# Moving the matrix transposes of a gated graph network from TensorE to 16-bit DMA transposes joined on ScalarE

## The chip, the core and the metric

The kernel runs on one core of a Trainium2 chip. The core has a matrix engine (TensorE, in the profile PE, with its weight loads shown as PEld), a vector engine (VectorE, DVE), an activation engine (ScalarE, ACT), a general engine (GpSimd, POOL) and a queue that here only issues DMAs (SyncE, SP). All engines run at once, each takes its own instructions strictly in order, and semaphores tie them together. The metric is the device time of one launch in microseconds (us); lower is better. Before the change it is 2248.63 us, the median of three runs between 2247.92 and 2249.76.

## What is computed

A batch of 64 graphs, each with 256 nodes and 256 features per node, goes through two layers. The first is a gated graph network with three rounds of message passing, the second an attention layer. Both see a normalized input and add their result to it.

```python
# x: (64, 256, 256) f32; adj: (64, 256, 256) int32, about 3% ones
h = relu(layernorm(x))
A = (adj != 0)
for i in range(3):                                   # layer 0
    m    = h @ weight[i]
    aggr = einsum('bst,bsd->btd', A, m)              # sum over source nodes
    gi, gh = aggr @ w_ih.T + b_ih, h @ w_hh.T + b_hh
    r = sigmoid(gi_r + gh_r);  z = sigmoid(gi_z + gh_z)
    n = tanh(gi_n + r * gh_n)
    h = (1 - z) * n + z * h
x = x + h
h = relu(layernorm(x))                               # layer 1
h1 = h @ W.T
e = leaky_relu((h1 @ a_left)[:, :, None] + (h1 @ a_right)[:, None, :])
alpha = softmax(where(adj == 0, -1e9, e))
out = x + alpha @ h1
```

Two layouts of the state h are needed. The gate products contract over features, so they need h with features on the partitions. Message passing contracts over source nodes, so it needs h with nodes on the partitions. Between rounds the state must therefore be transposed, as must the attention weights before they multiply h.

## The kernel before

Two graphs form a pair, and 32 pairs are worked one after the other, up to four of them open at once (WINDOW). A tile is 128 partitions by 512 f32 columns (256 KB): 28 general tiles ("full"), 32 of the rounded type fp32r ("round"), and the eight banks of PSUM. The names in the profile are these classes.

For each pair the stages are:

- Loading x and adj, layernorm and relu (`norm_relu`), and splitting the node-layout state into a rounded part hi and a remainder lo, so that message passing (`prop`, L541) runs as two fp32r products. Before round 0 the normalized state is also transposed into feature layout (`turn`, L523) and copied out of PSUM by ScalarE (L527).
- Three rounds. In each, the feature-layout state (hT, one tile for each of two feature blocks) and the propagated sum are cut into three rounded pieces by `split` (L440 to L443). Twelve or six matmuls of 128x512 for each gate and feature block follow in `gate`: the "top" products (L456), a scaling of the bank by ScalarE (L470), then the "rest" products (L461). Each round has 72 such matmuls for a pair, 36 for each feature block. Sigmoid, tanh and the update of hT in place (L572 to L574) follow on ScalarE and VectorE.
- After each round, the updated hT is transposed back to node layout (`back`, L584), for each graph four 128x128 transposes into one bank. After rounds 0 and 1, ScalarE rounds the bank to hi (L591) and VectorE forms lo (L592); after round 2, VectorE adds the bank to x (`res`, L589).
- Layernorm of the result and attention: scores, mask, exponential (L633). The weights are transposed by TensorE (`p turn`, L648), copied out (L652), multiplied by the state (`mix`, L657), projected (L666), scaled and added, and stored.

No engine's order is written by hand. Every operation is recorded in a `Plan` with an engine, an occupancy and a latency in ns, and the buffers that it reads and writes. `Plan.run` walks a clock and always places the operation that can start first; ties go by priority, which is a due time minus a hand-set lead (`LEAD`). The order so found is what each engine's queue holds. `in_turn` keeps the gates in a fixed interleaving: round 0 of pair p, round 2 of pair p-1, round 1 of pair p, round 0 of pair p+1, and so on. A wrong cost makes no wrong result, only another order. The occupancy constants of the plan are `MM, TR, PROP, PASS = 432, 109, 120, 232` and `A512, V512, S512, VP256, C512 = 470, 605, 660, 395, 530`; TR is one 128x128 transpose and PASS one 128x512 matmul. A DMA occupies SP in the plan for 5.6 ns per KB and lands 2200 ns later.

Of the kernel before, what the change touches and what calls it, by code (L numbers as in the profile page):

```python
# [10 lines left out]
F32 = mybir.dt.float32  # L11
F32R = mybir.dt.float32r
I32 = mybir.dt.int32
AF = mybir.ActivationFunctionType
# [9 lines left out]
    "w load": 3000, "load": 1000, "w 1": -20000, "G": -27000, "in 0 stats": -8000, "in 0 shift": 28000,  # L24
    "turn 1": 20000, "prop 0": -1000, "g1 d": -12000, "r 0 topF": 20000, "nh 0 topF": 4000, "ni 0 topF": 3000,
    "ni 0 rest": 9000, "z 0 topF": -6000, "z 0 rest": -3000, "r 1 topT": 1000, "nh 1 topF": -4000,
    "ni 1 topF": -5000, "z 1 topF": -22000, "back 0": 15000, "lo 0": -6000, "lo 1": 11000, "mid 0 stats": -15000,
    "mid 0 relu": -8000, "dot 0": -7000, "right 0": -15000, "project 0": -10000,
# [16 lines left out]
class Plan:  # L45
# [79 lines left out]
    def run(self, deadline):  # L125
# [16 lines left out]
        while done < len(self.ops):  # L142
            best = None
            for e, (free, avail) in engines.items():
                for o in avail:
                    if o.pair >= oldest + self.window and o.pair > 0:
                        continue
                    t = free
                    for q in o.preds:
                        t = max(t, q.start + q.occ if q.eng == e else q.end)  # L150
                    if o.port:
                        t = max(t, port["POOL" if e == "DVE" else "DVE"])
                    fits = True
                    for b in o.bufs:
                        if b.slot is None:
                            f = [s[0] for s in self.slots[b.cls] if s[2] is None]
                            if len(f) <= self.keep.get(b.cls, 0) * max(0, o.pair - max(oldest, 0)):
                                fits = False
                                break
                            t = max(t, min(f))  # L160
                    if fits and (best is None or (t, o.prio, o.seq) < best[0]):
                        best = ((t, o.prio, o.seq), o)
# [30 lines left out]
def tile_gated_gnn_then_gat(  # L193
# [82 lines left out]
    def dma(name, kb, fn, **kw):  # L276
        plan.op(name, "SP", kb * 5.6, kb * 5.6 + 2200, fn, **kw)
# [196 lines left out]

    def norm_relu(name, src, dst):
# [25 lines left out]
    def pair(p):  # L501
# [15 lines left out]
        for db in range(DB):  # L517
# [10 lines left out]

        for i in range(L):
# [4 lines left out]
            for db in range(DB):  # L534
                pa, ag = Buf("bank"), Buf("full")

                def prop(db=db, pa=pa, hi=hi, lo=lo):
                    for g in range(G):
                        terms = [(part[g], sb) for part in (hi, lo) for sb in range(NB)]
                        for n, (b, sb) in enumerate(terms):  # L540
                            nc.tensor.matmul(pa.t[:, ts(g, N)], parts(b)[:, sb, ts(db, P)], parts(A[g])[:, sb, :],  # L541
                                             start=(n == 0), stop=(n == len(terms) - 1))

                pe(f"prop {db}", 8 * PROP, prop, r=[(b, ONE) for b in hi + lo + A], w=[(pa, ONE)])
# [30 lines left out]

            if not last:
                hi, lo = [Buf("round") for _ in range(G)], [Buf("round") for _ in range(G)]
            for g in range(G):
                pt = Buf("bank")

                def back(g=g, pt=pt, hT=hT):
                    for nb in range(NB):
                        for db in range(DB):
                            nc.tensor.transpose(pt.t[:, (nb * DB + db) * P : (nb * DB + db + 1) * P],  # L584
                                                parts(hT[db])[:, g, ts(nb, P)], ident)

                pe(f"back {g}", 4 * TR, back, r=[(b, (g,)) for b in hT], w=[(pt, ONE)])
                if last:
                    dve(f"res {g}", V512, lambda b=XR[g], pt=pt: nc.vector.tensor_add(b.t, b.t, pt.t), r=[(pt, ONE)], w=[(XR[g], ALL)])  # L589
                else:  # L590
                    act(f"hi {g}", A512 + 10, lambda b=hi[g], pt=pt: nc.scalar.copy(b.t, pt.t), r=[(pt, ONE)], w=[(hi[g], ONE)])  # L591
                    dve(f"lo {g}", V512, lambda b=hi[g], c=lo[g], pt=pt: nc.vector.tensor_sub(c.t, pt.t, b.t.bitcast(F32)),  # L592
                        r=[(pt, ONE), (hi[g], ONE)], w=[(lo[g], ONE)])
# [45 lines left out]
        for g in range(G):  # L639
# [3 lines left out]
            pt, pT, pg, ag, pv = Buf("bank"), Buf("full"), Buf("bank"), Buf("full"), Buf("bank")  # L643

            def turn(g=g, pt=pt):
                for jb in range(NB):
                    for ib in range(NB):
                        nc.tensor.transpose(pt.t[:, (jb * NB + ib) * P : (jb * NB + ib + 1) * P],  # L648
                                            parts(pm_[g])[:, ib, ts(jb, P)], ident)

            pe(f"p turn {g}", 4 * TR, turn, r=[(pm_[g], ALL)], w=[(pt, ONE)])
            act(f"p copy {g}", A512, lambda pt=pt, pT=pT: nc.scalar.copy(pT.t, pt.t), r=[(pt, ONE)], w=[(pT, ONE)])  # L652

            def mix(g=g, pT=pT, pg=pg):
                for db in range(DB):
                    for jb in range(NB):
                        nc.tensor.matmul(pg.t[:, ts(db, N)], parts(hb[g])[:, jb, ts(db, P)], pT.t[:, ts(jb, N)],  # L657
                                         start=(jb == 0), stop=(jb == NB - 1))

            pe(f"mix {g}", 4 * MM, mix, r=[(pT, ONE), (hb[g], ALL)], w=[(pg, ONE)])  # L660
# [50 lines left out]
```

## Time and profile before

| | before |
|---|---|
| median of three runs | 2248.63 us |
| profiled execution, device time | 2247.52 us |
| its span, first to last instruction | 2245.7 us |
| one pair, span / 32 | 70.2 us |
| TensorE clock granted | 0.996 |

The profiled execution lies 1.1 us under the median, and its span 1.8 us under its own device time. A line of the groups reads: source line, engine, operation, output<-inputs by tile class, shape, xcount | busy us in total, mean ns of one | idle time just before, and what ended it. "Busy" of TensorE includes the drain of each matmul, so instructions that follow each other overlap: the distance from one start to the next, not the mean duration, is what one costs. In the timeline the columns are the start in us, the time from the first start to the last end of the group, engine, line, operation and count.

### The profile page before, as it was taken

To read this page: it belongs to the slowest core of one execution; us is meant where nothing else is said; L and a number is where in the kernel's file an instruction comes from. 1 tells how busy PE (TensorE), PEld (TensorE's weight loads), DVE (VectorE), ACT (ScalarE), POOL (GpSimd) and SP (SyncE) were. 2 spreads that over 40 slices of the span, in tenths; PEclk is the share of its full clock that TensorE was granted. 3 is DMA by queue.
4 is the path that set the end of the run, shared out by engine and by line. 5 is a ranking of instruction groups with operands and counts; after the bars stand their busy time and mean duration, and the time that the engine had idled before them with its cause. 6 is when DMAs were issued, how large, how long until landed. Compare 5 with 4: busy or idle time off the path is not lost.

```text
span 2245.7 us, 31163 instructions
## 1 busy us (share of the span) xinstructions
PE 2213.2 (99%) x10977; PEld 1822.5 (81%) x10977; DVE 1825.2 (81%) x4084; ACT 1662.8 (74%) x3069; POOL 140.6 (6%) x198
## 2 busy tenths in 40 slices
PE   8999999999999999999999999999999999999997
PEld 6788888888888888888888888888888888888875
DVE  7878877879878888778788778797787887787974
ACT  8677777777777777777777777777777777777764
POOL 1000000000000000000000000000000000000000
PEclk9999999999999999999999999999999999999998
DMA  3000111001111001110011110011110011100000
GB/s 103 20 20 29 38 38 38 20 20 38 38 39 34 24 20 38 38 38 29 15 33 39 38 38 20 20 39 38 38 34 24 20 38 38 38 29 15 15 19 28
DMA packets 72541, 71.75 MB, mean 32 GB/s; under 512 B 4272, under 2 KB 72384, under 8 KB 72384
## 3 DMA queue, kind: packets, MB, share of 16 engines
q1 hardware_dynamic: 72352, 69.75, 10.2%
q8 instruction: 86, 1.41, 0.3%
q14 instruction: 71, 0.58, 0.1%
q10 hardware_dynamic: 32, 0.01, 0.0%
HBM read 52.96 MB, written 16.78 MB: 31 GB/s over the span
## 4 chain that ended last, share of the span: by engine, by line
PE 70%; DVE 19%; ACT 8%; issue 3%; DMA 0%; ACTq 0%; POOL 0%; DVEq 0%; POOLq 0%
PE bank L456 32%; PE bank L461 16%; PE bank L541 5%; PE bank L657 5%; PE bank L666 5%; DVE round L442 4%; PE bank L584 3%; DVE round L443 3%; ACT full L496 2%; DVE full L314 2%; DVE full L574 2%; DVE full L573 2%; ACT bank L470 2%; DVE round L592 2%; PE bank L648 1%
## 5 line engine op out<-in xcount | busy, mean ns | idle before, releaser
L456 PE MATMUL bank<-round,fac_hh 128*128 128x512 f32 x2304 | 635.0, 402 | 0.5 <-DVE round L442 0.5
L456 PE MATMUL bank<-round,fac 128*128 128x512 f32 x2304 | 600.3, 395 | 0.0
L456 PEld LDWEIGHTS bank<-round,fac 128*128 128x128 f32 x2304 | 433.2, 188 | 103.4
L456 PEld LDWEIGHTS bank<-round,fac_hh 128*128 128x128 f32 x2304 | 410.7, 189 | 74.3 <-DVE round L442 1.0
L461 PE MATMUL bank<-round,fac_hh 128*128 128x512 f32 x1152 | 383.0, 413 | 0.7 <-ACT bank L470 0.7
L470 ACT ACTIVATE bank<-bank 128x512 f32<-128x512 f32 x576 | 327.5, 579 | 62.5 <-PE bank L456 62.3
L461 PE MATMUL bank<-round,fac 128*128 128x512 f32 x1152 | 355.5, 398 | 1.0 <-ACT bank L470 1.0
L441 ACT CAST round<-full 128x512 fp32r<-128x512 f32 x384 | 238.3, 621 | 156.9 <-DVE full L314 156.9
L442 DVE TENSOR_TENSOR round<-full,full 128x512 fp32r<-128x512 f32 x384 | 259.5, 689 | 8.7
L573 DVE TENSOR_TENSOR full<-full,full 128x512 f32<-128x512 f32 x192 | 129.3, 686 | 168.6 <-ACT full L567 168.5
L461 PEld LDWEIGHTS bank<-round,fac 128*128 128x128 f32 x1152 | 210.2, 188 | 61.9 <-ACT bank L470 16.4
L443 DVE SCALAR_TENSOR_TENSOR round<-round,full 128x512 fp32r<-128x512 f32 x384 | 255.5, 686 | 3.4
L461 PEld LDWEIGHTS bank<-round,fac_hh 128*128 128x128 f32 x1152 | 202.0, 189 | 48.5 <-ACT bank L470 16.4
L541 PEld LDWEIGHTS bank<-round,round 128*128 128x128 f32 x1536 | 204.7, 189 | 14.2 <-DVE round L592 0.9
L541 PE MATMUL bank<-round,round 128*128 128x256 f32 x1536 | 214.9, 285 | 0.7 <-DVE round L592 0.7
L572 DVE TENSOR_TENSOR full<-full,full 128x512 f32<-128x512 f32 x192 | 128.3, 681 | 106.4 <-ACT full L564 106.4
L490 POOL TENSOR_TENSOR small<-small,nhalf 128x2 f32<-128x2 f32 x128 | 106.1, 829 | 1477.6 <-DVE small L488 1476.8
L567 ACT ACTIVATE full<-bank,b_rz 128x512 f32<-128x512 f32 x192 | 132.2, 689 | 71.4 <-PE bank L461 71.1
L545 ACT COPY full<-bank 128x512 f32<-128x512 f32 x192 | 112.9, 588 | 88.2 <-PE bank L541 88.2
L314 DVE TENSOR_SCALAR full<-full 128x512 int32<-128x512 int32 (+1 forms) x400 | 161.7, 418 | 6.5 <-ACT full L545 5.0
L563 DVE TENSOR_TENSOR full<-full,bank 128x512 f32<-128x512 f32 x192 | 131.9, 687 | 40.8 <-PE bank L461 31.4
L556 ACT ACTIVATE full<-bank,b_rz 128x512 f32<-128x512 f32 x192 | 131.2, 684 | 40.4 <-PE bank L461 40.1
(74 smaller groups left out, 2723.0 us busy)
## 6 DMA issues: line engine op xcount, KB each, us to landing
x<-in_x_dram SPq DMA_DIRECT2D x64, 256.0 KB, 2.7
adj<-in_adj_dram SPq DMA_DIRECT2D x64, 256.0 KB, 2.7
full<-in_x_dram SPq DMA_DIRECT2D x64, 256.0 KB, 3.1
out_dram<-full SPq DMA_DIRECT2D x64, 256.0 KB, 2.2
full<-in_L_gnn_w_ih_dram SPq DMA_DIRECT2D x3, 256.0 KB, 4.2
full<-in_L_gnn_weight_dram SPq DMA_DIRECT2D x3, 256.0 KB, 4.6
full<-in_L_gnn_w_hh_dram SPq DMA_DIRECT2D x3, 256.0 KB, 5.3
full<-in_L_gnn_W_dram SPq DMA_DIRECT2D x1, 256.0 KB
```

Of the source, the lines that this page charges most:

```text
L314: dve2(name, 60 + n * 0.54, lambda: nc.vector.tensor_scalar(dst().bitcast(I32), src().bitcast(I32), CUT, None, op0=ALU.bitwise_and), r=r, w=w)
L441: act(name + " 0", C512, lambda: nc.scalar.copy(v0.t, t.t), r=[(t, ONE)], w=[(v0, ONE)])
L442: dve2(name + " 1", V512, lambda: nc.vector.tensor_sub(v1.t, v.t, t.t), r=[(v, ALL), (t, ONE)], w=[(v1, ONE)])
L443: dve2(name + " d", V512, lambda: nc.vector.scalar_tensor_tensor(vd.t, v1.t.bitcast(F32), -SPLIT, t.t, op0=ALU.mult, op1=ALU.add), r=[(v1, ...
L456: nc.tensor.matmul(bank.t, f(m, j, kb), b.t, start=(first and n == 0), stop=True, skip_group_check=True)
L461: nc.tensor.matmul(bank.t, f(m, 2, kb), s[kb][2].t, start=False, stop=True, skip_group_check=True)
L470: act(name + " scale", A512, lambda: nc.scalar.activation(bank.t, bank.t, AF.Identity, bias=bias, scale=1.0 + C), r=[("vec", ONE)], w=[(ba ...
L541: nc.tensor.matmul(pa.t[:, ts(g, N)], parts(b)[:, sb, ts(db, P)], parts(A[g])[:, sb, :], start=(n == 0), stop=(n == len(terms) - 1))
L556: act(f"r {db}", 575, lambda b=r_, k=pr, db=db: nc.scalar.activation(b.t, k.t, AF.Sigmoid, bias=b_rz[:, db : db + 1]), r=[(pr, ONE), ("b_r ...
L563: dve(f"u add {db}", V512, lambda u=u, k=pn: nc.vector.tensor_add(u.t, u.t, k.t), r=[(pn, ONE)], w=[(u, ONE)])
L567: act(f"z {db}", 575, lambda b=z_, k=pz, db=db: nc.scalar.activation(b.t, k.t, AF.Sigmoid, bias=b_rz[:, DB + db : DB + db + 1]), r=[(pz, O ...
L573: dve2(f"d mul {db}", V512, lambda d=d, b=z_: nc.vector.tensor_mul(d.t, d.t, b.t), r=[(z_, ONE)], w=[(d, ALL)])
```

## The change

Where the state or the attention weights were transposed by TensorE into a PSUM bank, a DMA now does it, for every pair but the first (its `turn`) and the last (its `back` and `p turn`).

The DMA transpose works on 16-bit elements. `dma_turn` views a tile of 512 f32 columns as 1024 columns of 16 bits, and one DMA transposes its eight 128x128 blocks. The rows that come out belong alternately to the lower and the upper halves of the f32 features. Two plain DMAs ("gather") then bring the 64 feature rows of each half of the partitions together so that the low halves of a row form one plane and the high halves another. Last, ScalarE interleaves the two planes into f32 again (`join`), a copy of 1024 16-bit elements for each partition. For `turn` each transposed tile holds both feature blocks of one graph, so it takes two gathers (four DMAs); for `back` and `p turn` one gather (two DMAs) suffices. In one pair that makes 10 DMA transposes, 24 gather DMAs and 10 joins. They live in SBUF tiles of the class "full", whose number is still 28.

`back` works by feature block instead of by graph: one transpose takes hT[db] with both graphs. hi and lo are therefore also held by feature block from round 1 on, `prop db` waits only for its own block, and `res` becomes four 128x256 additions for a pair instead of two of 128x512. hi is rounded from SBUF instead of PSUM. The attention weights keep the order that comes out of the transpose, and `mix` reads them with a stride.

In the plan, an SP operation that depends on another SP operation now waits for its landing (before, only for its issue), a load occupies SP for 600 ns instead of 1434, and all leads are set anew, so the order on every engine changes.

```diff
-            t = max(t, q.start + q.occ if q.eng == e else q.end)
+            t = max(t, q.start + q.occ if q.eng == e != "SP" else q.end)
...
-        plan.op(name, "SP", kb * 5.6, kb * 5.6 + 2200, fn, **kw)
+        plan.op(name, "SP", 600, kb * 5.6 + 2000, fn, **kw)
...
+    def dma_turn(name, src, t, gathers):
+        view = lambda q, blocks: t.t.bitcast(U16).rearrange("p (k q n) -> p q k n", q=2, n=P)[:, q, blocks, :]
+        plan.op(name, "SP", 1370, 3500, lambda: nc.sync.dma_start_transpose(
+            t.t.bitcast(U16).rearrange("p (c n) -> p c n", n=P), src.t.bitcast(U16)), r=[(src, ALL)], w=[(t, ALL)])
+        def gather(dst, blocks):
+            for q in range(2):
+                nc.sync.dma_start(dst(slice(64 * q, 64 * q + 64)), view(q, blocks))
+        for region, dst, blocks in gathers:
+            plan.op(name + " gather", "SP", 1320, 3200, lambda dst=dst, blocks=blocks: gather(dst, blocks),
+                    r=[(t, ALL)], w=[region])
+
+    def join(name, src, dst, order="b j n"):
+        act(name, 1100, lambda: nc.scalar.copy(
+            dst.t.bitcast(U16).rearrange("p (j n b) -> p j n b", j=2, b=2),
+            src.t.bitcast(U16).rearrange(f"p ({order}) -> p j n b", j=2, b=2)), r=[(src, ALL)], w=[(dst, ALL)])
...
-        for db in range(DB):
+        if p > 0:
+            rs = [Buf("full") for _ in range(DB)]
+            for g in range(G):
+                dma_turn(f"turn {g}", h[g], hT[g], [((rs[db], (g,)), lambda rows, g=g, b=rs[db]: b.t[rows].bitcast(U16).rearrange(
+                    "p (g b k n) -> p g b k n", g=G, b=2, k=NB)[:, g], slice(db, None, DB)) for db in range(DB)])
+            for db in range(DB):
+                join(f"turn copy {db}", rs[db], hT[db], "j b n")
+        for db in range(DB if p == 0 else 0):
...
+        far = p < NPAIR - 1
...
-                pe(f"prop {db}", 8 * PROP, prop, r=[(b, ONE) for b in hi + lo + A], w=[(pa, ONE)])
+                pe(f"prop {db}", 8 * PROP, prop, r=[(b, ONE) for b in (hi + lo if i == 0 else [hi[db], lo[db]]) + A], w=[(pa, ONE)])
...
-            for g in range(G):
-                pt = Buf("bank")
-                def back(g=g, pt=pt, hT=hT):
...
+            for db in range(DB):
+                hn = Buf("full" if far else "bank")
+                if far:
+                    rs = Buf("full")
+                    dma_turn(f"back {db}", hT[db], hn, [((rs, ALL), planes(rs), slice(None))])
+                    join(f"back copy {db}", rs, hn)
+                else:
...
-            pe(f"p turn {g}", 4 * TR, turn, r=[(pm_[g], ALL)], w=[(pt, ONE)])
-            act(f"p copy {g}", A512, lambda pt=pt, pT=pT: nc.scalar.copy(pT.t, pt.t), r=[(pt, ONE)], w=[(pT, ONE)])
+            if p < NPAIR - 1:
+                rs = Buf("full")
+                dma_turn(f"p turn {g}", pm_[g], pT, [((rs, ALL), planes(rs), slice(None))])
+                join(f"p copy {g}", rs, pT)
+            else:
+                pe(f"p turn {g}", 4 * TR, turn, r=[(pm_[g], ALL)], w=[(pt, ONE)])
+                act(f"p copy {g}", A512, lambda pt=pt, pT=pT: nc.scalar.copy(pT.t, pt.t), r=[(pt, ONE)], w=[(pT, ALL)])
```

## The prediction

> **What bounds the kernel now.** I read the page's busy shares first, then what TensorE waits for, then the timeline of TensorE for the price of one instruction.
>
> ```profile
> PE 2213.2 (99%) x10977; PEld 1822.5 (81%) x10977; DVE 1825.2 (81%) x4084; ACT 1662.8 (74%) x3069; POOL 140.6 (6%) x198
> ```
>
> TensorE is busy for 99% of the span, VectorE and ScalarE have 420 and 580 us to spare. A busy TensorE is not yet a bound, so I look at what it waits for (who waited, for whom, us in total, times, longest):
>
> ```profile
> PE bank L584 <- DVE full L574: 7.2, 15, 2.8
> PE bank L617 <- DVE full L606: 5.9, 3, 5.0
> PE bank L331 <- DMA rows<-in_L_gnn_b_hh_dram: 4.5, 1, 4.5
> PE bank L648 <- ACT full L633: 3.0, 1, 3.0
> PE bank L461 <- ACT bank L470: 1.7, 4, 0.7
> ```
>
> All its waits together are some 25 us, and 11 of them stand before the transposes that the change takes away (L584, L648, and 0.9 at L523). The start spacing confirms that TensorE's own rate is the limit:
>
> ```profile
> 1008.55 0.63 PE L461 MATMUL bank<-round,fac_hh 128*128 128x512 f32 x2
> 1009.01 0.60 PE L584 MATMUL bank<-ident,full 128*128 128x128 f32 x4
> 1009.37 1.17 PE L456 MATMUL bank<-round,fac_hh 128*128 128x512 f32 x4
> ...
> 1016.08 1.10 PE L456 MATMUL bank<-round,fac 128*128 128x512 f32 x4
> 1017.01 1.10 PE L456 MATMUL bank<-round,fac_hh 128*128 128x512 f32 x4
> ```
>
> Four matmuls of 128x512 take 0.93 us from start to start (1016.08 to 1017.01), 232 ns each. From 1008.55 to the instruction after these groups (1010.37 in the same view) are 1.82 us; two matmuls (0.46) and four (0.93) leave 0.43 us for four transposes: 108 ns each. The groups give the number of transposes, 768 + 256 + 256:
>
> ```profile
> L584 PE MATMUL bank<-ident,full 128*128 128x128 f32 x768 | 121.7, 274 | 9.8 <-DVE full L574 7.2
> L523 PE MATMUL bank<-ident,full 128*128 128x128 f32 x256 | 39.9, 278 | 0.9 <-ACT full L496 0.9
> L648 PE MATMUL bank<-ident,full 128*128 128x128 f32 x256 | 35.2, 282 | 3.1 <-ACT full L633 3.0
> L441 ACT CAST round<-full 128x512 fp32r<-128x512 f32 x384 | 238.3, 621 | 156.9 <-DVE full L314 156.9
> x<-in_x_dram SPq DMA_DIRECT2D x64, 256.0 KB, 2.7
> q1 hardware_dynamic: 72352, 69.75, 10.2%
> ```
>
> Their mean of 274 ns is latency, not cost. The last three lines are for the new operations: a ScalarE pass from SBUF, a 256 KB load that lands 2.7 us after issue, and the packets: 10.2% of 16 engines x 2245.7 us over 72,352 packets is 50.7 ns for each, nearly all of 1 KB.
>
> **What the Trainium skill says.** "ScalarE: Activation LUTs", What ACT_TABLE_LOAD costs: an ACTIVATE without pointer operands takes 186 + 0.833 N ns, and back-to-back ones overlap by 93. For N = 512 that is 613 alone; the trace has 621 (L441), so they agree. "DMA: Bandwidth & Descriptors", Latency and other measured facts, gives a DMA transpose 261 GB/s, or 350 to 400 if contiguous; its section Why small descriptors are slow (HBM only) says that copies inside SBUF with 128-byte packets still reach 78% of the bandwidth. The trace of before has neither. Its section Two DMAs through the same engine are not ordered says that a DMA that reads what another wrote must wait for that one's semaphore at the issuing engine; so SP stands still at each gather, and what is behind it stands too. The trace shows such a standing SP: at L674 it waited 1564.5 us for L671, at no cost, since nothing urgent was behind it.
>
> **The change, part by part.**
>
> *TensorE, removed.* `turn` goes for 31 pairs (8 transposes each), `back` for 31 (24 each), `p turn` for 31 (8 each): 31 x 40 = 1240 transposes x 108 ns = 134 us. All stand on the engine that bounds. No matmul is added; `mix` reads its moving operand with a stride of 512 bytes between runs of 128 columns, and I take that at its 216 ns spacing now (if it cost a tenth more, 512 x 22 ns = 11 us). The waits before the transposes, up to 11 us, may go or reappear at `prop`.
>
> *ScalarE.* For a pair, 10 joins come and 4 copies of 0.59 us (L527, L652) go; four hi passes now read SBUF, 621 instead of 581 ns. A join has N = 1024: 186 + 853 = 1.04 us alone, an estimate by the page that the trace supports at N = 512. The plan's 1.10 us is close, and its other costs have proved to be spacings in this trace (232, 109), so I take 1.0 to 1.1. Busy time for a pair: 1662.8 / 32 = 52.0, + 10.4 - 2.4 + 0.2 = 60.2 us. The bound on the other side is strided 16-bit access at half rate, 1.9 us a join, 69 us for a pair. But busy time counts the 93 ns overlap of some 91 instructions (8.5 us) twice, so ScalarE needs 52 us, or 60 at half rate. Below the 66 us that TensorE will need; no bound, but less air.
>
> *VectorE.* Four additions of 128x256 (0.34 us spacing, as L606) for two of 128x512 (0.60): +0.2 us a pair on 57. Nothing, below TensorE's 66.
>
> *SP.* For a pair 10 transposes, 24 gather DMAs and 8 loads and stores. An issue of a load takes 0.37 us in the trace. Gathers lie between that and the plan's 0.66; for the transposes I know no measured issue, so 0.4 to 2 us, and take the plan's 1.37. Sum 10 x 1.37 + 24 x 0.66 + 8 x 0.6 = 34 us of 66, at the worst 41. SP is no bound by occupancy; what counts is its standing in order.
>
> *DMA engines.* A transpose reads 128 x 8 runs of 256 bytes, and so does each round of gathers: 20 x 1024 = 20,480 packets for a pair. At 78% of 27 GB/s for each engine (an estimate from that page and its Specifications) a packet takes 12 ns, in all 15 us over 16 engines, beside 229 / 32 = 7 us of loads. At the 50.7 ns of a 1 KB packet it would be 65 us, 72 with the loads. I take the low end, since 256 bytes should not cost what 1024 cost from HBM; the high end is a rival.
>
> *The path.* Before: sigmoid, two products and sums on VectorE (0.69 each), 0.5 us transposes, hi and lo (1.3): about 4 us. After: the same, but 3.5 us to the transpose's landing, 3.2 for the gathers and 1.1 for the join instead of 0.5; the tail sigmoid to lo is then 0.7 + 1.4 + 7.8 + 1.3 = 11 us. The landings are estimates: the measured 2.7 for 256 KB from HBM, with one or two issues on top, and 1 us of data at 261 GB/s beside a fixed 2 us, come to the same 3 to 3.5. Cover: in the changed order of TensorE, counted at 232, 119 and 216 ns, 16 us of matmuls stand between the last gate product of a feature block after round 0 and the `prop` that needs it, and 21 us after round 1; of the first, 5 us are spare. Both pairs' other rounds are that cover. If the two landings together pass 11 to 12 us, TensorE stops. Queued behind a join that waits are the scalings L470, without which TensorE may not start a gate's rest products; queued behind a gather are loads, which have several us to spare.
>
> *Start and end.* The weights load first and x later; both orders have some 25 us of weight work on TensorE to fill the start, so I take 0 with 10 us either way. The last pair's end is as before.
>
> **Sum.** 2245.7 - 134 = 2112 for the span. For landings that come late now and then I add 0.2 us for each of the 62 shortened returns, 12 us: 2124. The median of the runs lies 2.9 us above the span: 2127 us.
>
> **Rivals.** *TensorE stays the bound* (forecast): 2100, where the old waits of 11 us go too, to 2165. For it: 25 us of waits in 2246, fixed spacings. Chance 0.60.
>
> *Half hidden.* Joins stand in ScalarE's order ahead of the scalings, ScalarE is 91% busy as the page counts, and a landing late by 1 us at ten joins delays a pair by perhaps 2: + 64 us, 2191, within 2165 to 2244. For it: 139 times TensorE's bank already keeps ScalarE waiting, so the two run close. Against: ScalarE has 66 - 52 = 14 us a pair to take it up. 0.14.
>
> *The DMAs bind, slower.* A 256-byte packet costs near what a 1 KB one costs. The place is the 16 DMA engines, the price 72.1 us for a pair, 32 x 72.1 = 2307, and with the ends some 2320. It decides from (66 - 7) x 16 / 20,480 = 46 ns a packet, or, seen from the path, where both landings together pass 13.3 us (the 16 us cover plus 2.2 us, which over 62 returns eat the 134). For it: the only packet price in the trace. Against: the page's small-packet figure. 0.23.
>
> *No effect.* If busy TensorE hid a ScalarE-to-TensorE round trip that paces the gates, removing transposes would only widen gaps: 2245. Against it: the 232 ns spacing right through. 0.03.
>
> **How the numbers follow.** The range 2100 to 2270 holds the first two, the no-effect case and a beginning of the slow one; about 0.03 lie below, 0.17 above. The likeliest case alone is 2100 to 2165. A change of 0.2% (4.5 us) is what this measurement can tell.
>
> **What would show it.** Right: 40 transposes left on TensorE besides the setup's and `right`; TensorE at 97% or more; few waits of `prop` or of PE on L470; joins of 1.0 to 1.1 us; transposes and gathers landing in 3 to 3.5 us; a DMA share near 35%. Wrong: TensorE waiting for lo at `prop` or ScalarE waiting for a DMA in most of the joins, DMA share over 80%, landings above 6 us.

## The result, and the profile after

The change had no effect that this measurement can tell. The median of four runs after is 2250.07 us (2246.3 to 2251.46), that of the four runs of the kernel before beside them 2249.2 us (2247.92 to 2250.17). The ratio is 1.0002, with a 95% interval of 0.9984 to 1.0019. The prediction was 2127 us.

The page of the kernel after, busy time of each engine, the line of the DMA queue that carries the data, and the shares of the chain of work that ended last:

```profile
PE 2129.9 (95%) x9737; PEld 1704.2 (76%) x9737; DVE 1865.9 (83%) x4148; ACT 1915.6 (85%) x3255; POOL 128.0 (6%) x198
...
q1 hardware_dynamic: 729056, 232.36, 56.7%
...
PE 32%; ACT 24%; DVE 17%; DMA 16%; issue 6%; SPq 5%; ACTq 0%; DVEq 0%
```

TensorE has exactly the 1240 transposes fewer (10977 to 9737) and is busy for 95% of the span, not 99%. The span is 2249.0 us (2245.7 before). The chain tells more than the busy share. In the kernel before it was:

```profile
PE 70%; DVE 19%; ACT 8%; issue 3%; DMA 0%; ACTq 0%; POOL 0%; DVEq 0%; POOLq 0%
```

Before, 70% of it ran through TensorE; now it is 32%, and ScalarE, the DMAs and SP have taken most of the rest. So the work went and something else is waited for. What TensorE waits for, in the same form as before (who waited, for whom, us in total, times, longest):

```profile
PE bank L463 <- ACT bank L472: 71.9, 90, 3.1
PE bank L458 <- ACT full L593: 15.6, 30, 0.5
...
PE bank L578 <- ACT round L635: 2.7, 3, 1.1
PE bank L578 <- DVE round L636: 2.6, 4, 1.1
```

L463 is the second part of a gate product, `rest` (L461 before), and L472 the scaling on ScalarE that must come between it and the first part (L470 before). That wait was 1.7 us in all and is 71.9. The place where one would look first, `prop` (L578), which needs the state that the DMAs bring back, waits for 5.3 us only. Why the scaling is late stands among the waits of all engines:

```profile
PEld bank L463 <- ACT bank L472: 147.3, 228, 3.6
DVE full L597 <- ACT full L593: 128.1, 62, 4.0
...
ACT full L496 <- DMA full<-full: 81.6, 75, 3.5
```

The first of these lines counts TensorE's weight loads, the second VectorE. ScalarE stands for 81.6 us before joins (L496) whose gather has not landed. One such place in time order, first ScalarE and then TensorE (start in us, duration, engine, line, operation; in brackets the idle time before it and who ended it):

```profile
1018.77 0.62 ACT L443 CAST round<-full 128x512 fp32r<-128x512 f32 x1 [0.29 <-DVE full L316]
1022.25 1.16 ACT L496 COPY full<-full 128x1024 uint16<-128x1024 uint16 x1 [2.86 <-DMA full<-full]
1023.32 0.68 ACT L593 ACTIVATE full<-bank,b_rz 128x512 f32<-128x512 f32 x1
1023.90 0.59 ACT L472 ACTIVATE bank<-bank 128x512 f32<-128x512 f32 x1
```

```profile
1020.95 0.64 PE L463 MATMUL bank<-round,fac 128*128 128x512 f32 x2
1024.54 1.22 PE L463 MATMUL bank<-round,fac 128*128 128x512 f32 x2 [2.95 <-ACT bank L472]
1025.56 1.06 PE L458 MATMUL bank<-round,fac_hh 128*128 128x512 f32 x2
```

ScalarE stands for 2.86 us before the join. Behind it wait a sigmoid (L593) and a scaling (L472), neither of which needs the join's data. They start when the join has run, at 1023.32 and 1023.90, and 0.05 us after the scaling's end, at 1024.54, TensorE starts again: it has stood for 2.95 us. VectorE waits behind the sigmoid in the same way (L597).

The stop has a tail. The two matmuls behind it take 1.02 us from start to start (1024.54 to 1025.56), where 0.46 is usual, and the trace's record of the granted clock shows half of the full clock for 3.4 us from 1024.4 on. Between 200 and 2000 us of this run there are five such stretches, 20.5 us together, and each begins within 1.2 us of the end of a stop of TensorE of 1.9 to 3.1 us. The kernel before has none there. That the stop brings the lower clock is suggested by this, not shown. As an estimate from these figures, the five cost some 10 us of TensorE's time.

Matched by the order of ScalarE's queue, most of the standing lies before two of the ten joins of a pair: that of block 0 after round 2 (31 waits, 34.5 us), and that of block 1 after round 0 (30 waits, 34.8 us). The other eight share 14.5 us.

### The profile page after: what moved, and what is told of

It is laid out like the page before. It is cut to its first block, busy times and chain, and to the rows that moved or that the text cites. A ratio compares the mean times of both kernels' runs of the same rounds, so it can differ in the third digit from the quotient of the medians.

```text
span 2249.0 us, 31172 instructions
## 1 busy us (share of the span) xinstructions
PE 2129.9 (95%) x9737; PEld 1704.2 (76%) x9737; DVE 1865.9 (83%) x4148; ACT 1915.6 (85%) x3255; POOL 128.0 (6%) x198
## 4 chain that ended last, share of the span: by engine, by line
PE 32%; ACT 24%; DVE 17%; DMA 16%; issue 6%; SPq 5%; ACTq 0%; DVEq 0%
PE bank L458 18%; DMA full<-full 16%; PE bank L463 9%; ACT full L496 5%; ACT bank L472 4%; SPq L488 4%; ACT full L593 2%; ACT round L443 2%; DVE round L444 2%; DVE round L445 2%; DVE full L316 2%; PE bank L717 2%; ACT full L524 2%; ACT full L604 2%; DVE round L636 1%
## 5 line engine op out<-in xcount | busy, mean ns | idle before, releaser
L458 PE MATMUL bank<-round,fac_hh 128*128 128x512 f32 x2304 | 624.3, 400 | 19.9 <-ACT full L593 15.6
L458 PE MATMUL bank<-round,fac 128*128 128x512 f32 x2304 | 618.7, 400 | 0.3 <-ACT round L443 0.3
L458 PEld LDWEIGHTS bank<-round,fac_hh 128*128 128x128 f32 x2304 | 432.0, 190 | 129.7 <-ACT full L593 28.7
L458 PEld LDWEIGHTS bank<-round,fac 128*128 128x128 f32 x2304 | 433.2, 189 | 100.0 <-ACT round L443 0.7
L496 ACT COPY full<-full 128x1024 uint16<-128x1024 uint16 x310 | 362.2, 1169 | 83.9 <-DMA full<-full 81.6
L463 PE MATMUL bank<-round,fac_hh 128*128 128x512 f32 x1152 | 377.2, 413 | 35.6 <-ACT bank L472 35.3
L463 PE MATMUL bank<-round,fac 128*128 128x512 f32 x1152 | 360.4, 403 | 36.6 <-ACT bank L472 36.6
L472 ACT ACTIVATE bank<-bank 128x512 f32<-128x512 f32 x576 | 334.2, 584 | 24.9 <-PE bank L458 21.6
L463 PEld LDWEIGHTS bank<-round,fac 128*128 128x128 f32 x1152 | 212.8, 190 | 104.6 <-ACT bank L472 59.8
L463 PEld LDWEIGHTS bank<-round,fac_hh 128*128 128x128 f32 x1152 | 199.5, 188 | 117.4 <-ACT bank L472 87.4
L444 DVE TENSOR_TENSOR round<-full,full 128x512 fp32r<-128x512 f32 x384 | 265.5, 692 | 16.9 <-DVE full L316 0.5
L445 DVE SCALAR_TENSOR_TENSOR round<-round,full 128x512 fp32r<-128x512 f32 x384 | 261.7, 688 | 10.5
L597 DVE TENSOR_TENSOR full<-bank,full 128x512 f32<-128x512 f32 x192 | 132.1, 688 | 137.1 <-ACT full L593 128.1
L578 PEld LDWEIGHTS bank<-round,round 128*128 128x128 f32 x1536 | 205.7, 190 | 22.3 <-ACT round L635 4.2
L578 PE MATMUL bank<-round,round 128*128 128x256 f32 x1536 | 211.9, 283 | 6.0 <-ACT round L635 2.7
L518 POOL TENSOR_TENSOR small<-small,nhalf 128x2 f32<-128x2 f32 x128 | 97.5, 762 | 2093.1 <-DVE small L516 1746.7
L316 DVE TENSOR_SCALAR full<-full 128x512 int32<-128x512 int32 (+1 forms) x400 | 166.7, 418 | 22.5 <-ACT full L582 16.1
L472 ACT ACTIVATE bank<-bank,vec 128x512 f32<-128x512 f32 x192 | 124.1, 657 | 60.7 <-PE bank L458 60.7
```

The lines of the kernel that those rows point to most:

```text
L316: dve2(name, 60 + n * 0.54, lambda: nc.vector.tensor_scalar(dst().bitcast(I32), src().bitcast(I32), CUT, None, op0=ALU.bitwise_and), r=r, w=w)
L444: dve2(name + " 1", V512, lambda: nc.vector.tensor_sub(v1.t, v.t, t.t), r=[(v, ALL), (t, ONE)], w=[(v1, ONE)])
L445: dve2(name + " d", V512, lambda: nc.vector.scalar_tensor_tensor(vd.t, v1.t.bitcast(F32), -SPLIT, t.t, op0=ALU.mult, op1=ALU.add), r=[(v1, ...
L458: nc.tensor.matmul(bank.t, f(m, j, kb), b.t, start=(first and n == 0), stop=True, skip_group_check=True)
L463: nc.tensor.matmul(bank.t, f(m, 2, kb), s[kb][2].t, start=False, stop=True, skip_group_check=True)
L472: act(name + " scale", A512, lambda: nc.scalar.activation(bank.t, bank.t, AF.Identity, bias=bias, scale=1.0 + C), r=[("vec", ONE)], w=[(ba ...
```

## The experiments

The theory, H below: a join that waits in ScalarE's order for a landing holds up the sigmoids and scalings behind it, and TensorE stands for those. The main rival, P: the way of the state back to `prop` has become longer than its cover, so TensorE loses the time wherever the join stands. A second rival, L: the work of the joins alone, some 10 us of ScalarE for a pair, delays the scalings. Each experiment changes the kernel after. Its ratio is to the kernel before, run beside it, where the changed kernel itself stands at 1.0002.

### Nothing waits for a landing

```diff
-        view = lambda q, blocks: t.t.bitcast(U16)...
+        view = lambda q, blocks: fac["hh"][:, 0, 0, :GN].bitcast(U16)...
...
-            dst.t.bitcast(U16)..., src.t.bitcast(U16)...), r=[(src, ALL)], w=[(dst, ALL)])
+            src.t.bitcast(U16)..., blank.bitcast(U16)...to_broadcast(...)), r=[(src, ALL)], w=[(dst, ALL), (src, ALL)])
```

The gathers here read a constant and write the transpose's own tile, and what follows reads the tile that the join fills with a constant. So DMAs, joins and their order stay, and nothing is transposed.

> The joins, in the same place of ScalarE's order and of the same size, read a constant tile and write the tile that consumers read, so none waits for the transpose or gather before it; DMAs are as many and as large, SP's order the same (the output is not the reference's: the transposed data are replaced by a constant). Theory H (ScalarE stands at joins whose data have not landed, and the scalings L472 behind them hold TensorE): ScalarE's idle time before joins falls from 82 us to under 20, TensorE's waits on L472 (72 us) to under 20, time 2120 to 2170. Theory L (the 10 us a pair of join work on ScalarE alone delays the scalings): nothing changes, 2235 to 2255. Theory P (the return path is too long and TensorE waits for the state) also expects a gain, but of the few us that prop waits show.

2161.25 us (2159.55 to 2162.32), ratio 0.9609 [0.9594, 0.9623]. Its page and what TensorE waited for (lines are one or two higher here):

```profile
PE 2110.7 (98%) x9737; PEld 1699.2 (79%) x9737; DVE 1857.8 (86%) x4149; ACT 1872.3 (87%) x3255; POOL 128.1 (6%) x198
```

```profile
PE bank L459 <- ACT full L595: 15.5, 30, 0.5
...
PE bank L464 <- ACT bank L473: 3.8, 7, 1.3
```

With the same instructions in the same order (and one memset more) and the same number of DMAs, the span falls from 2249.0 to 2160.2 us, 88.8 us. TensorE's wait for scalings falls from 71.9 to 3.8 us, and ScalarE has no wait for a DMA left at a join. The waits for landings cost nearly all of the 88.8: the joins are also quicker here (starts 0.94 us apart instead of 1.065; they read a constant), and by the price of join work that the next run gives, that is some 6 us of it. Transfers and issues that merely run beside the kernel are thus not what costs, nor is SP's standing by itself: SP still waits 143.5 us for landings at its gathers (153.0 in the kernel after).

Of the 88.8 us, 69.6 are TensorE standing less (span without busy time, 119.1 and 49.5 us). In the other 19.2 us it was busy longer in the kernel after with the same instructions; about half of that is the estimate of 10 us for the five stretches of lower clock, which are absent here. The data are constants here, and whether that alone changes the clock was not tested. L, which expected 2235 or more, is out as the main cause. P as it was put for this run expected only the few us that `prop` waits; if the way back delays TensorE through the other engines too, it would give this gain as H does. So the order must be moved to tell the two apart.

The same kernel with joins of 512 f32 elements, 0.42 us shorter each:

```diff
-            src.t.bitcast(U16)..., blank.bitcast(U16)...to_broadcast([P, 2, GN // 2, 2]))
+            parts(src), blank...to_broadcast([P, 2, GN // 2]))
```

> As the run whose joins wait for no landing (2161 us), same order, but each join copies 512 f32 instead of 1024 16-bit elements (0.52 instead of 0.94 us a join, 130 us less of ScalarE; the transposed data are replaced by a constant as there). Theory L in its remaining part (the 49 us between 2161 and the 2112 of the sum are the join's work): 2125 to 2140. If TensorE bounds there already: within 8 us of 2161.

2143.59 us (2142.76 to 2144.96), 0.9534 [0.9521, 0.9547], a little above what L's remaining part expected. The span is 2140.7 us, 19.5 less. So 310 x 0.42 = 130 us of ScalarE's work are worth 19.5 us of the span: ScalarE's occupancy is the smaller part of the loss. What is left over the 2112 us that TensorE's own work was predicted to take is 29 us; 15.5 of it are 30 waits of 0.5 us of a first product (L458 in the kernel after) for a bank that a sigmoid still reads, one in each pair.

### Two moves in ScalarE's order

A pass behind the planner puts one operation, with what hangs on it, behind the next k of its engine; all else keeps its place. ("back copy 0", 2) is the join of block 0 after round 2.

```diff
+        plan.pass_on(order, {("back copy 0", 2): 2})                          # last join later
+        plan.pass_on(order, {("back copy 1", 0): 3})                          # first join later
+        plan.pass_on(order, {("back copy 0", 2): 2, ("back copy 1", 0): 3})   # both
```

> All orders as in the changed kernel, but on ScalarE the join of feature block 0 after round 2 (31 of them; 34.5 us of ScalarE's waits for DMAs stand before these) goes behind the next two instructions, a sigmoid and a scaling of the other pair. Nothing soon needs that join. Theory H: ScalarE no longer stands there, the scaling goes ahead: 20 to 45 us faster than the changed kernel, 2205 to 2230. Theory P (the length of the state's return path sets the time): no gain, within 6 us of 2250.

2233.93 us (2231.9 to 2236.22), 0.9936 [0.9924, 0.9949], 16 us less than the changed kernel. The waits, with lines 24 higher:

```profile
PE bank L487 <- ACT bank L496: 58.5, 87, 2.6
ACT full L520 <- DMA full<-full: 58.1, 58, 3.5
```

The standing before this join falls from 34.5 to 2.9 us. Some returns at the other places: 37.1 instead of 34.8 before block 1 after round 0, 7.2 instead of 1.1 before block 1 after round 2. P, which allowed 6 us, fails at this join. H has the direction, but not its size (it expected 20 to 45 us): ScalarE stands 23.5 us less in all (81.6 to 58.1), and the span is 14.6 us shorter (2249.0 to 2234.4). This join feeds only the residual sum (L632), which is not urgent, and its landing need not be waited for so early. It is the only version run that computes everything and beats both kernels.

> All orders as in the changed kernel, but the join of feature block 1 after round 0 and its hi pass go behind the next three instructions of ScalarE that do not hang on it (34.8 us of waits for DMAs stand before these joins). Theory H: 10 to 40 us faster than the changed kernel. Theory P: this join is on the return path of the state, so a later place makes it slower, 2255 to 2290.

2267.18 us (2265.21 to 2269.68), 1.0083 [1.007, 1.0097], 17 us more. The standing before this join is gone (34.8 to 0.1 us), and still the time rises:

```profile
PE bank L487 <- ACT bank L496: 91.1, 94, 2.7
...
DVE round L660 <- ACT round L659: 84.4, 37, 4.3
```

The same wait of VectorE in the kernel after:

```profile
DVE round L636 <- ACT round L635: 24.9, 19, 4.3
```

The join and its hi now come later: the join starts 14.4 us after the last gate product instead of 12.4, and `prop` at 17.8 instead of 17.0 (medians over the pairs). lo on VectorE (L636, here L660) keeps its place and now stands for hi: 84.4 us, against 24.9. The standing has moved from ScalarE's queue to VectorE's, and what VectorE holds back holds up ScalarE in turn: its tanh waits 49.5 us for VectorE's sum, against 3.2. H alone fails at this join: it is on the way back, as P says, and the time lies in P's range.

> Both moves at once. Theory H: the gains add, 2165 to 2210, near the run without landing waits (2161). Theory P: 2250 or slower.

2252.53 us (2249.36 to 2256.86, 12 runs), 1.0019 [1.0011, 1.0028]. The two moves add up, -16 and +17; H had expected 2165 to 2210. ScalarE's waits for landings are 22.8 us here, 58.8 less than in the kernel after, and nothing is gained: VectorE's lo stands 83.3 us for hi. So it is not ScalarE's standing as such that counts, but what ends up waiting for the landing.

### SP's order

After the transpose of block 1 in round 0, SP's queue holds in 28 pairs a store, the next pair's first `turn` transpose, a load, and only then this transpose's gather. In the timeline of SP of the kernel after (start, duration, line, operation, count):

```profile
997.98 1.27 SPq L483 DMA_TRANSPOSE full<-full  x1
999.35 0.53 SPq L725 DMA_DIRECT2D out_dram<-full  x1
999.98 1.28 SPq L483 DMA_TRANSPOSE full<-full  x1
1001.32 0.57 SPq L305 DMA_DIRECT2D x<-in_x_dram  x1
1001.98 1.30 SPq L488 DMA_DIRECT2D full<-full  x2
```

The gather is issued 4.0 us after the transpose (997.98 to 1001.98), while a landing takes 3.4.

```diff
+        plan.pass_on(order, {("turn 0", 0): 2})                               # gather first
+        plan.pass_on(order, {("turn 0", 0): 2, ("back copy 0", 2): 2})        # and last join later
+        plan.pass_on(order, {..., ("back copy 1", 2): 2})                     # and block 1's last join
```

> All orders as in the changed kernel, but on SP the gather of feature block 1 after round 0 goes ahead of the next pair's turn transpose and one load (28 pairs), so that it is issued when its own transpose has landed, about 0.7 us sooner. If SP's standing in order is part of the return path that stops ScalarE: the waits before that join (35 us) fall to under 20 and the kernel is 10 to 25 us faster than the changed one, 2225 to 2240. If the landing alone sets it: within 5 us of 2250.

2285.12 us (2283.96 to 2290.8), 1.0166 [1.0152, 1.018]. The aim was reached: this join starts at 11.4 us instead of 12.4, `prop` at 16.1 instead of 17.0, and the standing before the join falls from 34.8 to 8.9 us. But the time rises by 35 us, which was not expected: SP now stands for the landing with the `turn` behind it, and the standing before the join of `turn` rises from 4.1 to 65.2 us:

```profile
ACT full L520 <- DMA full<-full: 108.7, 72, 3.6
PE bank L487 <- ACT bank L496: 97.6, 92, 3.0
```

> The earlier gather on SP and the later join of block 0 after round 2 (alone: 2234) together, all else in the changed kernel's order. If the two standings are separate the gains add: 2205 to 2225; if they are one loop: 2225 to 2236.

2268.22 us (2266.88 to 2273.59), 1.0091 [1.0077, 1.0104].

> As before, and the join of block 1 after round 2 also goes behind the next two instructions of ScalarE (7 us of waits stood before it once the first had moved). 0 to 8 us faster than with two moves.

2289.53 us (2285.92 to 2291.46), 1.0177 [1.0163, 1.0191]. With the last join moved as well, the gain of that move (17 us) is there again, and the third move loses 21, where 0 to 8 us of gain were expected. None is faster than the single move of the last join.

### A second issuing queue

If SP's standing is what delays, GpSimd, busy for 6%, could issue some gathers. All three start from the kernel with the last join later (2233.93 us).

```diff
-                nc.sync.dma_start(dst(slice(64 * q, 64 * q + 64)), view(q, blocks))
+                (nc.gpsimd if name.startswith("turn") else nc.sync).dma_start(...)   # turn
+                nc.gpsimd.dma_start(...)                                             # all
+                (nc.gpsimd if name.startswith("back") else nc.sync).dma_start(...)   # back
```

> Orders as in the run with the later last join (2234), but the eight gather DMAs of turn for a pair are issued from GpSimd's queue instead of SP's, which frees 5.2 us of SP a pair just ahead of the transposes after round 2. If the one SP queue is what makes landings late: the joins' waits for DMAs fall from 58 to under 40 us, 2200 to 2228. If landing times alone count, or the GpSimd issue costs as much: 2228 to 2245; slower if pow stands behind these gathers.

2252.62 us (2249.4 to 2266.4, 22 runs), 1.0022 [1.0014, 1.003].

> As the run before, but all 24 gathers of a pair come from GpSimd's queue, so SP stands at none. If SP's queue is the cause: 2170 to 2215. If a gather issued from GpSimd lands over 1 us later than from SP, the return path is longer and this is slower than 2234.

2341.13 us (2335.06 to 2348.07), 1.0419 [1.0399, 1.044].

> Only the gathers of back come from GpSimd's queue, those of turn and of the attention weights stay on SP. If SP's standing before the gather of the return path (0.7 us at block 1 after round 0) and behind the turn gathers counts: 2205 to 2230. If a GpSimd gather lands later: 2240 to 2290.

2318.36 us (2305.74 to 2328.08), 1.0309 [1.0283, 1.0335]. The gathers of `turn`, in the kernel after and in the first of these runs (queue, count, KB each, median us from issue to landing):

```profile
full<-full SPq DMA_DIRECT2D x248, 64.0 KB, 2.2
```

```profile
full<-full POOLq DMA_DIRECT2D x248, 64.0 KB, 3.3
```

The 64 KB gathers land 1.1 us later when GpSimd issues them. The standing before the first join of `turn` is 31.0 us, against 4.3. In the other two it is block 1 after round 0 that stands, for 94.6 and 90.0 us, against 37.1. The 128 KB gathers as a whole land no later by much there (medians 3.7 and 3.5 us, 3.5 from SP), but at that place the join starts 6.4 and 6.3 us after the second gather's issue, against 3.8; why just these are late is not shown. The Trainium skill, "DMA: Bandwidth & Descriptors", Issuing engines are not separate DMA queues, says that a second issuing engine saves only the time to issue, since all DMAs run on the same 16 engines. The runs agree that nothing is won, and go further: here it cost from 19 to 107 us, with the gathers of `turn` and of `back` alone more than was expected.

### The parts undone or planned anew

Four runs let the planner make a new order. They bear on the question less, since every engine's order changes with them.

```diff
-        plan.op(name, "SP", 1370, 3500, ...          # late plan: both landings 1.5 us later
+        plan.op(name, "SP", 1370, 5000, ...
...
-            plan.op(name + " gather", "SP", 1320, 3200, ...
+            plan.op(name + " gather", "SP", 1320, 4700, ...
...
-        far = p < NPAIR - 1                          # back on TensorE
+        far = False
...
-        act(name, 1100, lambda: nc.scalar.copy(      # joins on GpSimd
+        pool(name, 1100, lambda: nc.gpsimd.tensor_copy(
```

> The plan is told that a transpose lands after 5.0 us and a gather after 4.7 us (instead of 3.5 and 3.2), so it puts joins later in ScalarE's order. Theory H: ScalarE waits less for DMAs (82 us to under 30), TensorE less for L472; 2180 to 2230, less what a longer return path costs. Theory L: within 10 us of 2250. Theory P: slower, 2260 or more, since the path gets longer.

2362.04 us (2361.22 to 2363.71), 1.0503 [1.0486, 1.0521]. Of the expectations, P's came true. ScalarE's waits for DMAs at joins fell from 81.6 to 6.5 us, but TensorE's for scalings rose:

```profile
PE bank L463 <- ACT bank L472: 118.9, 109, 3.8
```

The joins hardly stand any more, and `prop` starts 22 to 25 us after the last gate product. TensorE's granted clock was 0.961 in this run, against 0.989. The lowered stretches are all at half clock in the record, so it ran at half clock for 184 us of the span against some 49; by this estimate up to (184 - 49) / 2 = 67 of the 112 us lie there. Telling the planner of later landings did not mend the kernel by that alone. The landings that it was told here (5.0 and 4.7 us) are longer than the measured ones (3.4 and some 4.2, see below), and no run gave it those. As a test of H it failed: it changed more than it meant to.

> back goes to TensorE again for all pairs (by feature block, copied from PSUM), turn and p turn stay by DMA with 4 joins a pair. TensorE gets 31 x 24 x 108 ns = 80 us back. Theory H: the four joins left have long slack, TensorE's waits on L472 fall to the 10 us of before, so 2250 - 110 + 80 = 2200 to 2225. Theory L: the waits fall with the join work to 40 percent of what was added, 2250 - 60 + 80 = 2255 to 2275.

2259.13 us (2258.25 to 2259.64), 1.0044 [1.0029, 1.0059]. With the 24 transposes of `back` for a pair on TensorE again, TensorE waited 27.4 us for scalings. That is less than 71.9, as H says, and 31 x 24 x 108 ns = 80 us of work are back on TensorE; but the order was planned with leads that were set for another kernel, and the time lies in L's range (2255 to 2275), not in H's, so this one is inconclusive.

> The joins are copies on GpSimd instead of ScalarE, all else as in the changed kernel; the plan orders anew. Theory H and L: ScalarE has neither the joins nor their waits, so TensorE's waits on the scalings go, 2120 to 2180, if a join on GpSimd takes under 2 us and does not hold VectorE. Theory P: no gain, since the return path is not shorter; above 2240. If GpSimd takes over 3 us a join or holds VectorE's port, the path or VectorE binds, above 2260.

2397.73 us (2393.91 to 2402.28), 1.0662 [1.0646, 1.0678]. H and L had expected a gain. The standing went to GpSimd, where little else stands behind it, and the time still rose: a join there takes 1.27 us, VectorE is slowed, and the granted clock was 0.963. How much each of these weighs was not taken apart. The same group of VectorE, first in the kernel after and then here:

```profile
L611 DVE TENSOR_TENSOR full<-full,full 128x512 f32<-128x512 f32 x192 | 132.6, 691 | 5.5
```

```profile
L611 DVE TENSOR_TENSOR full<-full,full 128x512 f32<-128x512 f32 x192 | 153.6, 800 | 6.0
```

> The changed kernel with the plan's leads of the kernel before, so another order on every engine and the same work. If the order is what holds the standings down, this is slower by far, 2300 to 2450; if the order matters little: within 20 us of 2250.

The fourth gives the changed kernel the leads of the kernel before: 2326.4 us (2322.18 to 2326.91), 1.0341 [1.0327, 1.0355]. The leads that came with the change are worth 76 us to it, so the loss does not come from worse leads than before.

## Why the prediction was wrong

**The step that failed** is the term for waits in the sum: "for landings that come late now and then I add 0.2 us for each of the 62 shortened returns, 12 us". Measured, it is 88.8 us, of which some 6 belong to the longer joins, so about 1.3 us for each of the 62 returns. The price is paid little at `prop` (5.3 us of waits) and mostly at the scalings (71.9 us). Its companion, the rival "Half hidden", named the mechanism, joins ahead of the scalings in ScalarE's order, and gave it a chance of 0.14. It was priced at ten joins late by 1 us, delaying a pair by 2 us. In fact mainly two joins of a pair are late, by 1.1 us each in the mean, and with the landings' waits gone a pair is 2.7 us shorter. That the 83 us of loss come near the 81.6 us of standing is in part chance: 68 us of the loss are TensorE's waits for scalings, the rest slower running and other waits, and the moves of single joins returned less than the standing that they removed. "Against: ScalarE has 66 - 52 = 14 us a pair to take it up" was the wrong argument all the same. Idle time of an engine in the mean doesn't help an instruction that is queued behind a wait: in the lines shown the scaling ran when the join was through, and TensorE started again only 0.05 us after the scaling.

**The path of 11 us** is a term that was mis-sized. For block 1 after round 0, medians from the end of the last gate product: the sigmoid ends at 2.2 us (0.7 in the prediction; it starts 1.5 us late in ScalarE's queue) and the last sum is ready at 3.7 (2.1). The gather is issued 4.1 us after the transpose (3.5), because of what stands ahead of it on SP. The join starts 4.5 us after that (3.2): a gather is two DMAs of 128 KB, the second issued 0.65 us after the first, and landing 3.5 us after its own issue in the median of all. That makes 4.2 us from the first issue where the plan, too, had 3.2; the difference is about what the two joins are late by, but no run tested this link. hi and lo end at 15.0. The path is 15 us, not 11, against a cover of 16: of the "5 us spare" one was left. `prop` itself starts at 17.0, two after lo: TensorE reaches it late after its other stops, and the state is there. With the join later hi and lo end at 16.9, the spare is gone, and 17 us were lost. With the gather sooner the path was shorter, `prop` started at 16.1, and the 35 us were lost at `turn`.

**TensorE, -134 us:** right. 1240 transposes are gone, 40 are left beside the setup's and `right`, matmuls still start 232 ns apart outside the stretches of lower clock, and where nothing waits for landings and joins are short the span comes down to 2140.7 us. 29 us remain over the predicted 2112; 15.5 of them are the bank waits named above, the other 13 were not taken apart.

**ScalarE:** right as a price; the conclusion left the waits out. Joins start 1.065 us apart (1.0 to 1.1 predicted), and its busy time for a pair is 1915.6 / 32 = 59.9 us (60.2). "No bound, but less air" holds for occupancy: shortening every join by 0.42 us returned 19.5 us.

**SP:** 31 us of issues for a pair by the trace (34 predicted): 1.28 for a transpose, 0.61 for a gather DMA. That it "is no bound by occupancy; what counts is its standing in order" was right. But the standing was given no price, neither on SP nor on ScalarE.

**DMAs:** the transpose lands after 3.4 us (3.5 predicted). Packets of 256 bytes took 26 ns in the mean, not the 12 that the prediction worked out from the 78% of the Trainium skill ("DMA: Bandwidth & Descriptors", Why small descriptors are slow (HBM only)), which is stated there for a 1 MB remote transfer; the share was 57%, not 35. By the prediction's own terms the two landings' limit of 13.3 us should have been 13.7 (16 + 2.2 - 4.5), which decides nothing. The loss with binding DMAs (0.23) did not come, since 26 is below the 46 ns from which it decides. The run without waits for landings, with the same DMAs, shows that their load alone costs little.

**No effect (0.03)** has the right time by chance and the wrong reason. It supposed a round trip hidden under TensorE already before; but with the landings' waits gone, TensorE follows the removal of its transposes at once, to 98% busy. The wait is new. That it came out at just no change is two unrelated amounts, 134 us of work and some 137 us of loss, that happen to meet.

What stays open: how much of the 83 us a wholly different order could regain, and how the 83 us divide between ScalarE's order, the length of the way back and the clock. One move gave 16. All orders that the planner made anew were worse, and no order was searched for by hand beyond the moves shown.

## What to carry to other kernels

A wait for a DMA that an engine takes on in its order holds up whatever is queued behind it, however much that engine idles in the mean: price such a change by what stands behind the waiting instruction and who waits for that. The idle time alone is no price: of two joins with the same 35 us of standing, moving one gained 16 us and moving the other lost 17. Add up a moved path from issue to issue, with the queue ahead of each issue and the last of several DMAs, before it is set against its cover. When testing, move one instruction in a fixed order: what a planner makes of a changed cost mixes the cause with a new order.

## What the hardware showed that was not expected

- A gather of 64 KB inside SBUF landed 2.2 us after its issue from SP and 3.3 us from GpSimd. By the queue's line below (packets, MB, share of 16 engines) it moved from GpSimd in 7,936 packets for 16.27 MB (2 KB each) instead of 256 bytes each, and was still not sooner. For gathers of 128 KB the medians are 3.5 us from SP and 3.5 to 3.7 from GpSimd.

```profile
q0 software_dynamic: 7936, 16.27, 2.9%
```

- Copies on GpSimd slow VectorE where it reads two operands from SBUF: 691 to 800 ns. Its operation with one operand in PSUM (L597) stayed at 686 (688 in the kernel after). An operation with a single operand, in SBUF (L316), rose too, from 418 to 459, so the second operand is not all of it. The Trainium skill, "SBUF — State Buffer", SBUF: two separate sides, says that a VectorE operation with two SBUF inputs and a GpSimd one that reads SBUF lock each other out; the rise of L611 and the steady L597 agree with that, and no run here shows what holds L316.
- A 16-bit copy of 1024 elements with strides takes 1169 ns on ScalarE, and 1042 where it reads a broadcast constant instead. The 1.04 us worked out beforehand fits the second. The two lines are of the kernel after and of the run in which nothing waits for a landing:

```profile
L496 ACT COPY full<-full 128x1024 uint16<-128x1024 uint16 x310 | 362.2, 1169 | 83.9 <-DMA full<-full 81.6
L497 ACT COPY full<-blank 128x1024 uint16<-128x1024 uint16 x310 | 322.6, 1042 | 0.0
```

- By the record of the granted clock, TensorE ran at half of its clock for 3.4 to 6.8 us at a time, around the end of five of its stops of 1.9 to 3.1 us in the middle of the kernel after. The estimate above, some 10 us, is a part of the loss that no list of waits shows.
